# A graph network in one plan: setup reordered, later sign check, GpSimd booked longer, new priorities

## The chip, the cores and the metric

The kernel runs on one core of a Trainium2 chip. The metric is the device time of one execution in microseconds (us). The engines of the core are called PE (TensorE, matrix products), DVE (VectorE), ACT (ScalarE), POOL (GpSimd) and SP (SyncE, which here only issues transfers).

## The reference

Sixteen inputs of 1024 nodes with 256 features pass four layers over one 1024 x 1024 adjacency matrix of integers. Each layer adds its result to `x`, and each starts from `relu(layernorm(x))`. Layers 0 to 2 are graph attention, layer 3 is a transformer block:

```python
q = h @ W                                   # layer 0: 4 heads of 64; layers 1, 2: 1 head of 256
e = leaky(q @ a_src [i] + q @ a_dst [j])
x = x + act(softmax(where(adj > 0, e, -big)) @ q)     # elu, relu, elu
# layer 3: 8 heads of 32
t = softmax(where(adj > 0, q k^T / sqrt(32), -big)) @ v
y = layernorm(h + t);  y = layernorm(y + relu(y @ w1 + b1) @ w2 + b2);  x = x + y
```

## The kernel before

One core does all sixteen batches. `direct` does not emit instructions at once: it records pieces of work (`rec.add`) with an engine, an estimated duration and the buffers read and written. `Record.schedule` then plays a list schedule over the engines with these estimates and emits the pieces in the order that comes out. Each engine so has one fixed order, and semaphores on the buffers do the rest. Among the pieces ready on an engine the smallest key goes first. A key is the batch number plus a curve (`KNOTS`) over the position in its stream; `LEAD` shifts ACT's and DVE's keys, `BIAS` times `SWITCH` favours staying in PE's present packing, `PASS` is what passes until another engine sees a result, `SLACK` the same for transfers. A stream with a last argument of False has no lead.

The stages, by line of the kernel before:

- `setup` records `prepare(0)`, eight `neighbours`, `prepare(1)`, `prepare(2)` and the loads of the last layer's weights. `prepare` loads a layer's weights and multiplies them with the attention vector (DVE, L585 to L614). `neighbours` loads 128 rows of `adj` into a tile of `pa` (L623), makes flags of them in a second `pa` tile (DVE, L628), turns them on PE (L531) and copies them as bytes into `mask` (ACT, L646); DVE takes the least value of each row for a sign check (L655). The ring `r_pa` has six tiles.
- `begin` loads a batch (L1608) and takes sums and squares for its first layer norm on ACT (L1618, L448).
- `gat` is one graph layer. The inverse root is a power on POOL (L468 after squares, L483 after variances), DVE combines it with the mean (L475, L492), ACT writes the normalised rows `hn` (L502), PE turns them (L531) and multiplies with `w_aug` (L772). The exponentials `e` go through `rt` and `rd` and come back from memory spread over all partitions as `row` (L845, L854). DVE makes the weights `pt` (L870) from `row`, `e` and `mask`; PE multiplies them, in layer 0 by four column-packed matmuls at once (L984, L994), in layers 1 and 2 in 257 columns (L897, followed by DVE's reciprocal L917). POOL adds `e` to a running sum (L822).
- `attention` makes `qs` and `ks` (L1134 onwards), scores on PE (L1363) into four `sc` banks, exponentials on ACT (L1387), masks on DVE (L1396) and column-packed products with `va` (L1220). The tile `ks` is free until then.
- `feed` is the two-layer network of layer 3 (L1460) and the last layer norm.

The two first batches run layer 0 side by side; the second borrows tiles of the later layers for it (`lent`: `hTa`, `yT`, `xr`, `sums`, `pa`). After that every batch's graph layers are interleaved with the attention of an earlier one. All loads and stores but the running sums of `pa` (POOL, L1264) go through SP's queue, in the order of the plan.

Of the kernel before, what the change touches and what calls it, by code (L numbers as in the profile page):

```python
# [113 lines left out]


WEIGHT = {"pe": 1.0, "dve": 0.3}
PASS = {"pe": 0.146, "act": 0.223, "dve": 0.215, "pool": 0.13, "dma": 0.0}


class Work:  # L120
# [23 lines left out]
class Record:  # L144
# [135 lines left out]


BEHIND, HELD = 2.0, 1.35
SLACK = 0.871
KNOTS = {
    "gat0": (-9.618, -6.053, -5.32, -5.141, -2.375, -3.129, -0.814, -6.083, -6.096),
    "gat1": (-0.417, 0.283, 0.48, 0.671, 0.58, 0.798, 0.823, 0.86, 0.875),
    "gat2": (1.011, 0.044, -0.065, -1.338, 0.793, 0.704, 0.959, 1.386, 1.211),
    "beside": (-2.107, 2.085, 1.792, -1.66, 7.109),
    "values": (-0.174, -0.634, -1.621, -1.921, -0.925, 0.988, 7.017, 0.066, 0.002),
    "steps": (0.679, 1.306, 1.313, 1.627, 1.731, 1.892, 2.245, 2.072, 0.464),  # L290
    "feed": (2.531, 3.778, 2.14, 2.018, 2.622, 2.047, -0.257, 0.785, 3.186),
    "last": (1.057, 1.904, 1.664, 0.156, 2.035, 2.203, 2.695, 3.982, 5.043),
}
BIAS = 2.353
LEAD = {"act": 5.778, "dve": -2.572}

SWITCH = {
    ("full", "col4"): 0.137,
# [30 lines left out]
def direct(ctx, tc, flag, x, adj, gat_w, gat_a, w_qkv, ln1_g, ln1_b, ln2_g, ln2_b, w1, b1, w2, b2, out):  # L329
# [99 lines left out]
    def pool(us, emit, w, r):  # L429
        rec.add("pool", us, emit, w, r)  # L430

    def dma(moved, lands, emit, w, r, key=None, us=0.57, engine="dma"):
        rec.add(engine, us, emit, w, r, key=key, moved=moved, lands=lands)

    def stats(src, src_ref, dst, dst_ref, whose="g"):
# [19 lines left out]
    def inverse_of_squares(mean, squares, rstd, refs, rstd_ref, negate=True):  # L455

        n = squares.shape[-1]
        dve(
            ts_us(n),
            lambda: nc.vector.tensor_scalar(  # L460
                rstd, squares, 1.0 / C, EPS, op0=ALU.mult, op1=ALU.add
            ),
            [rstd_ref],
            refs,
        )
        pool(
            0.98,
            lambda: nc.gpsimd.tensor_tensor(  # L468
                out=rstd, in0=rstd, in1=neg_half[:, :n], op=ALU.pow
            ),  # L470
            [rstd_ref],
            [],
        )
        if negate:
            dve(tt_us(n), lambda: nc.vector.tensor_mul(mean, mean, rstd), refs, [rstd_ref])  # L475

    def inverse(mean, var, rstd, mv_refs, rstd_ref, negate=True):

        n = var.shape[-1]
        dve(ts_us(n), lambda: nc.vector.tensor_scalar_add(rstd, var, EPS), [rstd_ref], mv_refs)  # L480
        pool(
            0.98,
            lambda: nc.gpsimd.tensor_tensor(  # L483
                out=rstd, in0=rstd, in1=neg_half[:, :n], op=ALU.pow
            ),
            [rstd_ref],
            [],
        )
        if negate:
            dve(  # L490
                stt_us(n),
                lambda: nc.vector.scalar_tensor_tensor(  # L492
                    mean, mean, -1.0, rstd, op0=ALU.mult, op1=ALU.mult
                ),
                mv_refs,
                [rstd_ref],
            )
# [49 lines left out]


    b_aug = [Buf(t, []) for t in w_aug]
    b_mask, b_least, b_qkv, b_feed = (Buf(t, []) for t in (mask, least, wqkv_sb, w1_sb))  # L550

    def prepare(l):

        H = HEADS[l]
        D = C // H
        a_bc, aug = r_ota.new(), b_aug[l]
        dma(
            1.2,
            2.0,
            lambda: nc.sync.dma_start(  # L560
                w_aug[l][:, :, :C], gat_w[l].rearrange("(t p) d -> p t d", p=P)
            ),
            [aug],
            [],
        )
        dma(
            0.5,
            1.8,
            lambda: nc.sync.dma_start(
                a_bc.t.rearrange("p (s d) -> p s d", s=2)[:, :, :D],  # L570
                bass.AP(
                    tensor=gat_a[l].tensor, offset=gat_a[l].offset, ap=[[0, P], [D, 2], [1, D]]
                ),
            ),
            [a_bc],
            [],
        )
        for ct in range(CT):
            for s in range(2):
                tmp = r_ex.new()  # L580
                prod = tmp.t[:, :C].rearrange("p (h d) -> p h d", h=H)
                a_s = a_bc.t[:, s * C : s * C + D].rearrange("p (o d) -> p o d", o=1)
                dve(
                    tt_us(C),
                    lambda: nc.vector.tensor_mul(  # L585
                        prod,
                        w_aug[l][:, ct, :C].rearrange("p (h d) -> p h d", h=H),
                        a_s.to_broadcast([P, H, D]),
                    ),
                    [tmp],  # L590
                    [aug, a_bc],
                )
                to = C + (1 - s) * H
                dve(
                    tt_us(C),
                    lambda: nc.vector.tensor_reduce(
                        w_aug[l][:, ct, to : to + H], prod, AX.X, ALU.add
                    ),
                    [aug(("score", ct, s))],
                    [tmp],  # L600
                )
            wd = w_aug[l][:, ct, C : C + H]
            ws = w_aug[l][:, ct, C + H : C + 2 * H]
            dve(
                0.06,
                lambda: nc.vector.tensor_scalar_mul(
                    w_aug[l][:, ct, C + 2 * H : C + 3 * H], wd, ALPHA[l] - 1.0
                ),
                [aug(("low", ct))],
                [aug(("score", ct, 1))],  # L610
            )
            dve(
                0.06,
                lambda: nc.vector.tensor_scalar_mul(ws, ws, 1.0 - ALPHA[l]),  # L614
                [aug(("score", ct, 0))],
                [],
            )

    def neighbours(it):
        a32, nat = r_pa.new(), r_pa.new()  # L620
        a_i = a32.t.rearrange("p a n -> p (a n)").bitcast(I32)
        dma(
            1.8, 1.7, lambda: nc.sync.dma_start(a_i, adj[it * P : (it + 1) * P, :]), [a32], []  # L623
        )
        nat_f = nat.t.rearrange("p a n -> p (a n)")
        dve(
            ts_us(N),
            lambda: nc.vector.tensor_scalar(nat_f, a_i, 0.0, None, ALU.is_gt),  # L628
            [nat],
            [a32],  # L630
        )
        for j0 in range(0, NT, TH):
# [6 lines left out]
                    TH,  # L639
                ),  # L640
                [g],
                [nat],
            )
            act(
                act_us(HALF),
# [4 lines left out]
                [b_mask((it, j0))],  # L650
                [g],
            )
        dve(
            tt_us(N),
            lambda: nc.vector.tensor_reduce(least[:, it : it + 1], a_i, AX.X, ALU.min),  # L655
            [b_least(it)],
            [a32],
        )

    def mask_of(hf):  # L660
        return [b_mask((it, j0)) for it in range(hf * TH, (hf + 1) * TH) for j0 in (0, TH)]

    def setup():
        rec.stream(-3.0, (0.0, 1.0), False)
        prepare(0)
        rec.stream(-0.9, (0.0, 0.1), False)
        for it in range(NT):
            neighbours(it)
        rec.stream(-0.5, (0.0, 0.3), False)
        prepare(1)  # L670
        prepare(2)
# [2 lines left out]
            2.5,  # L674
            lambda: nc.sync.dma_start(wqkv_sb, w_qkv.rearrange("(t p) d -> p t d", p=P)),
            [b_qkv],
            [],
        )

        def load_feed():  # L680
# [4 lines left out]
            for n, ap in (("g2", ln2_g), ("c2", ln2_b)):  # L685
                nc.sync.dma_start(rows[n][:, 0, :], rows_on_all(ap, C))

        dma(5.0, 2.5, load_feed, [b_feed], [], us=5.7)

# [32 lines left out]
        )  # L724
        return rings

    def gat(xt, b_mv, b_rstd, l, my):
        H = HEADS[l]
        D = C // H
        mv, rstd = b_mv.t, b_rstd.t  # L730
# [5 lines left out]
        for hf in range(2):  # L736
            s = slice(hf * TH, (hf + 1) * TH)
            its = range(hf * TH, (hf + 1) * TH)
            mv_refs, rstd_ref = [b_mv((l, it)) for it in its], b_rstd((l, hf))
            inv = inverse_of_squares if l in SQUARED else inverse  # L740
            inv(mv[:, l, s, 0], mv[:, l, s, 1], rstd[:, l, s], mv_refs, rstd_ref)
            hn, hT = my.hn.new(), my.hT.new()
            for k, it in enumerate(its):
# [69 lines left out]
            if H == 1:  # L813
# [4 lines left out]
                    [b_e3(it) for it in its],  # L818
                )
            pool(  # L820
                0.686,
                lambda: nc.gpsimd.tensor_tensor(  # L822
                    out=sum_e[:, :, :H, s],
                    in0=sum_e[:, :, :H, s],
# [23 lines left out]
        def spread(hf, h, rd):  # L848
# [8 lines left out]
                    .rearrange("t n -> (t n)")  # L857
                    .partition_broadcast(P),
                ),
                [row],  # L860
                [rd],
            )
            return row

        def weights(hf, h, jt, row):
# [733 lines left out]
    def begin(b):  # L1599
        xt, b_mv, b_rstd = Halves(r_xh), r_mv.new(), r_rstd.new()  # L1600
        x_b = x[b].rearrange("(t p) c -> p t c", p=P)
        rec.stream(b, (0.0, 0.0), False)
        for hf in range(2):
            s = slice(hf * TH, (hf + 1) * TH)
            dma(
                1.8,
                3.0,
                lambda: nc.sync.dma_start(xt.half(hf), x_b[:, s, :]),  # L1608
                [xt(it) for it in range(hf * TH, (hf + 1) * TH)],
                [],  # L1610
                b - 1.0,
            )
        for hf in range(2):
            its = range(hf * TH, (hf + 1) * TH)
            for it in its:
                act(
                    act_us(C, 0, 1) + 95e-3,
# [13 lines left out]
            )  # L1631
        return xt, b_mv, b_rstd

    def graph(b, state, l, my=own, knots=None):
        rec.stream(b, knots or KNOTS[f"gat{l}"])
        gat(*state, l, my)

    def end(b, state):
        xt, x3 = state[0], r_x3.new()
# [11 lines left out]
        feed(b, x3, hn)  # L1651

    setup()
    states = [begin(0), begin(1)]
    graph(0, states[0], 0)
    borrowed = lent()
    graph(0, states[1], 0, borrowed, KNOTS["beside"])
    for r in vars(borrowed).values():
        if isinstance(r, Lent):
            r.give_back()  # L1660
    for b in range(NB):
        if b > 1:
            states.append(begin(b))
# [615 lines left out]
```

## Time and profile before

| | us |
|---|---|
| median of 3 runs | 4063.11 |
| lowest and highest | 4061.49, 4064.12 |
| the profiled execution | 4055.53 |
| its span | 4053.7 |
| PE busy in it | 3972.2 |
| DVE busy | 3624.3 |
| ACT busy | 2670.9 |
| POOL busy | 641.4 |

The span runs from the first to the last instruction of the core. The profile gives, for each engine, busy time, for each group of equal instructions its count, mean duration and the idle time just before it with the work that ended that idle time. The granted clock of PE was 0.997 of full speed over the span.

### The profile page before, as it was taken

The numbers are of one execution on the slowest core, as the hardware profiler recorded it, in microseconds if no ns is written. First come the engines' busy times: TensorE is split into PE (matmuls) and PEld (weight loads), VectorE is DVE, ScalarE is ACT, GpSimd is POOL, SyncE is SP. The second block draws the span as 40 slices with busy tenths as digits, with TensorE's granted clock in tenths as the row PEclk, the third lists the DMA queues.
The fourth block names the chain that finished last, engine by engine and source line by source line (L and its number), as shares of the span: only waits on it lengthen the run. The fifth ranks groups of instructions, "written<-read, shape, count | busy, mean of one in ns | idle before, by whom it ended". The sixth has DMA issues, their size and how long they took to land. (4 is left out here: it accounts for less than half of the span.)

```text
span 4053.7 us, 64966 instructions
## 1 busy us (share of the span) xinstructions
PE 3972.2 (98%) x23394; PEld 2337.5 (58%) x23394; DVE 3624.3 (89%) x6114; ACT 2670.9 (66%) x6673; POOL 641.4 (16%) x631
## 2 busy tenths in 40 slices
PE   7999999999999999999999999999999999999998
PEld 3566466564655646566565655646556465565653
DVE  7768998989989899999999989899898988989976
ACT  5467575675756766567675766757577665676675
POOL 1001121111112111111111211112021111211200
PEclk9999999999999999999999999999999999999999
DMA  4044453444544355453544535446444454535442
GB/s 129 24 118 110 119 137 98 120 104 117 138 106 117 92 128 123 111 135 80 136 111 120 136 90 129 99 117 141 103 115 99 122 129 107 134 82 124 117 127 57
DMA packets 227514, 456.46 MB, mean 113 GB/s; under 512 B 24688, under 2 KB 59760, under 8 KB 227184
## 3 DMA queue, kind: packets, MB, share of 16 engines
q1 hardware_dynamic: 192624, 326.39, 29.0%
q0 software_dynamic: 34560, 125.84, 16.2%
q8 instruction: 186, 3.05, 0.3%
q14 instruction: 144, 1.18, 0.1%
HBM read 225.25 MB, written 101.06 MB: 80 GB/s over the span
## 5 line engine op out<-in xcount | busy, mean ns | idle before, releaser
L1396 DVE TENSOR_TENSOR pa<-pa,mask 128x1024 f32<-128x1024 f32 x1024 | 1223.4, 1216 | 106.4 <-ACT pa L1387 106.3
L1387 ACT ACTIVATE pa<-sc 128x512 f32<-128x512 f32 x2048 | 1092.2, 600 | 229.2 <-PE sc L1363 146.0
L870 DVE SCALAR_TENSOR_TENSOR pt<-row,e,mask 128x512 f32<-128x512 f32 x1472 | 1006.4, 741 | 39.7 <-DMA row<-rd 22.7
L897 PE MATMUL bank<-qb,pt 128*128 128x257 f32 x4096 | 942.6, 381 | 3.5 <-DVE pt L870 3.3
L897 PEld LDWEIGHTS bank<-qb,pt 128*128 128x128 f32 x4096 | 769.3, 189 | 178.6 <-ACT ota L1303 12.6
L1363 PE MATMUL sc<-qs,ks 128*128 128x512 f32 x2048 | 739.3, 463 | 3.5 <-ACT pa L1387 3.4
L1220 PE MATMUL bank<-pa,va 128*32 128x512 f32 x4096 | 518.4, 598 | 0.2
L1363 PEld LDWEIGHTS sc<-qs,ks 128*128 128x128 f32 x2048 | 366.5, 189 | 220.9 <-issue 93.0
L984 PE MATMUL bank<-pt,qb 128*32 128x512 f32 x3840 | 459.8, 595 | 0.0
L1264 POOL DMA_DIRECT2D sums<-pa x240 | 213.9, 892 | 1464.5 <-DVE pa L1396 664.4
L925 ACT ACTIVATE ex<-bank,rec 128x256 f32<-128x256 f32 x256 | 121.3, 474 | 409.1 <-DVE rec L917 403.3
L772 PE MATMUL bank<-w_aug,hT 128*128 128x259 f32 (+1 forms) x1504 | 373.8, 390 | 0.7 <-ACT hT L766 0.7
L772 PEld LDWEIGHTS bank<-w_aug,hT 128*128 128x128 f32 x1504 | 276.7, 190 | 112.9 <-issue 33.6
L1247 DVE TENSOR_TENSOR sums<-pa,pa 128x1024 f32<-128x1024 f32 x240 | 289.1, 1217 | 9.9 <-PE bank L1220 9.9
L1255 DVE TENSOR_TENSOR sums<-sums,pa 128x1024 f32<-128x1024 f32 x240 | 290.9, 1213 | 1.6 <-DMA sums<-pa 1.6
L984 PEld LDWEIGHTS bank<-pt,qb 128*32 128x32 f32 x3840 | 120.3, 109 | 264.1 <-issue 218.5
L994 PE MATMUL bank<-pt,e 128*32 128x512 f32 x1920 | 251.2, 592 | 0.0
L1015 ACT COPY ot<-bank 128x512 f32<-128x512 f32 x120 | 68.5, 582 | 276.0 <-PE bank L984 262.9
L1134 PE MATMUL sc<-hTa,wqkv_sb 128*128 128x512 f32 x512 | 245.0, 601 | 3.0 <-ACT pa L1387 2.7
L1220 PEld LDWEIGHTS bank<-pa,va 128*32 128x32 f32 x4096 | 110.3, 109 | 237.1 <-issue 206.8
L502 ACT ACTIVATE hn<-xh,mv,rstd 128x256 f32<-128x256 f32 x376 | 199.1, 607 | 42.7 <-DVE mv L492 38.2
L448 ACT ACTIVATE waste<-xh,mv 128x256 f32<-128x256 f32 x384 | 196.1, 511 | 7.2
(153 smaller groups left out, 4608.6 us busy)
## 6 DMA issues: line engine op xcount, KB each, us to landing
sums<-pa POOLq DMA_DIRECT2D x240, 512.0 KB, 4.9
ks<-hl SPq DMA_DIRECT2D x256, 256.0 KB
qs<-hl SPq DMA_DIRECT2D x256, 256.0 KB
row<-rd SPq DMA_DIRECT2D x184, 256.0 KB
hl<-hi SPq DMA_DIRECT2D x128, 256.0 KB
hl<-lo SPq DMA_DIRECT2D x128, 256.0 KB
xh<-in_x_dram SPq DMA_DIRECT2D x32, 512.0 KB
x<-xh SPq DMA_DIRECT2D x32, 512.0 KB
```

The costliest lines, as they stand in the source:

```text
L772: nc.tensor.matmul(g.t[:, : C + 3 * H], hT.t[:, ct, k * P : (k + 1) * P], w_aug[l][:, ct, :], start=ct == 0, stop=ct == CT - 1,)
L870: lambda: nc.vector.scalar_tensor_tensor(pt.t, row.t, e3[:, 2, jt // TH, h, jt % TH : jt % TH + 1], mask[:, jt, hf * HALF : (hf + 1) * HAL ...
L897: nc.tensor.matmul(g.t[:, : D + 1], pts[jt].t[:, k * P : (k + 1) * P], qb[:, jt, 0, :], start=jt == 0, stop=jt == NT - 1,)
L984: nc.tensor.matmul(g.t[u * D + d : u * D + d + D3, :], qb[:, j, h + u, d : d + D3], pts[u][j - jt].t, start=j == 0, stop=j == NT - 1,)
L994: nc.tensor.matmul(gd.t[c : c + D3, :], one(jt + k, h + u).to_broadcast([P, D3]), pts[u][k].t, start=jt == 0, stop=jt == NT - 2,)
L1134: nc.tensor.matmul(sc.t, wqkv_sb[:, ct, c0 : c0 + P], hT.t[:, ct, hf * HALF : (hf + 1) * HALF], start=ct == 0, stop=ct == CT - 1,)
L1220: nc.tensor.matmul(ac.t[r * D3 : (r + 1) * D3, :], columns(r), of_head(r), start=first, stop=last,)
L1247: lambda: nc.vector.tensor_add(ss.t, p0.t, p1.t),
L1255: lambda: nc.vector.tensor_add(ss.t, ss.t, pt.t),
L1363: nc.tensor.matmul(scs[r - r0].t, ks.t[:, r, jt * P : (jt + 1) * P].bitcast(F32R), q.t[:, r, :].bitcast(F32R), start=True, stop=True,)
L1387: lambda: nc.scalar.activation(pt.t[:, v, :], sc.t, AF.Exp, scale=1.0 / math.sqrt(D3)),
L1396: lambda: nc.vector.tensor_mul(pt.t, pt.t, mask[:, jt : jt + 1, i0 : i0 + HALF].to_broadcast([P, 2, HALF]),),
```

## The change

Setup. The flags of `neighbours` go into the four parts of the tile `ks`, written as FP32R, and no longer into `pa`. The least values are taken later, in `signs`, from a second load of `adj` into `yT` tiles. `prepare(1)`, `prepare(2)` and the weight loads move to `setup_later`, recorded after batch 0's layer 0, and these loads and those of batches 1 and 2 are made to wait until the second, fourth or eighth `row` transfer has landed (`AFTER_ROWS`). Batch 0 takes its first statistics on DVE with `stats`, so its first inverse root goes the way of `inverse` (L480, L483, L492).

Plan. POOL's powers are booked with 1.6 in place of 0.98 us and its sums of `e` with 1.0 in place of 0.686, an SP issue with 0.42 in place of 0.57. `PASS`, `SLACK`, `KNOTS`, `BIAS` and `LEAD` have new values.

```diff
@@ -114,7 +114,7 @@
 WEIGHT = {"pe": 1.0, "dve": 0.3}
-PASS = {"pe": 0.146, "act": 0.223, "dve": 0.215, "pool": 0.13, "dma": 0.0}
+PASS = {"pe": 0.198, "act": 0.161, "dve": 0.218, "pool": 0.13, "dma": 0.0}
 
@@ -280,19 +280,19 @@
 BEHIND, HELD = 2.0, 1.35
-SLACK = 0.871
+SLACK = 0.944
 KNOTS = {
-    "gat0": (-9.618, -6.053, -5.32, -5.141, -2.375, -3.129, -0.814, -6.083, -6.096),
-    "gat1": (-0.417, 0.283, 0.48, 0.671, 0.58, 0.798, 0.823, 0.86, 0.875),
-    "gat2": (1.011, 0.044, -0.065, -1.338, 0.793, 0.704, 0.959, 1.386, 1.211),
-    "beside": (-2.107, 2.085, 1.792, -1.66, 7.109),
-    "values": (-0.174, -0.634, -1.621, -1.921, -0.925, 0.988, 7.017, 0.066, 0.002),
-    "steps": (0.679, 1.306, 1.313, 1.627, 1.731, 1.892, 2.245, 2.072, 0.464),
-    "feed": (2.531, 3.778, 2.14, 2.018, 2.622, 2.047, -0.257, 0.785, 3.186),
-    "last": (1.057, 1.904, 1.664, 0.156, 2.035, 2.203, 2.695, 3.982, 5.043),
+    "gat0": (-8.057, -7.567, -4.564, -6.528, -1.817, -1.899, -1.452, -3.246, -8.552),
+    "gat1": (-2.024, -0.004, 0.215, 0.731, 0.959, 0.704, 0.611, 0.917, 0.899),
+    "gat2": (1.118, -0.917, 0.633, 0.85, 0.97, 0.804, 1.307, 1.739, 1.201),
+    "beside": (-0.565, 3.144, 4.806, -3.201, 8.62),
+    "values": (-3.421, -4.341, -3.452, -4.286, -2.082, -2.123, 4.475, -0.299, 0.523),
+    "steps": (-0.249, 0.878, 1.095, 1.509, 1.61, 1.967, 1.973, 2.318, 0.345),
+    "feed": (4.232, 4.502, 1.869, 1.3, 2.54, 0.571, -2.425, 2.126, 2.697),
+    "last": (4.663, 0.548, 4.755, 0.436, 4.627, 5.109, 4.463, 6.627, 6.529),
 }
-BIAS = 2.353
-LEAD = {"act": 5.778, "dve": -2.572}
+BIAS = 4.008
+LEAD = {"act": 4.014, "dve": -5.116}
 
@@ -429,7 +429,7 @@
 
-    def dma(moved, lands, emit, w, r, key=None, us=0.57, engine="dma"):
+    def dma(moved, lands, emit, w, r, key=None, us=0.42, engine="dma"):
         rec.add(engine, us, emit, w, r, key=key, moved=moved, lands=lands)
@@ -464,7 +464,7 @@
         pool(
-            0.98,
+            1.6,
             lambda: nc.gpsimd.tensor_tensor(
@@ -479,7 +479,7 @@
         pool(
-            0.98,
+            1.6,
             lambda: nc.gpsimd.tensor_tensor(
@@ -547,7 +547,11 @@
     b_aug = [Buf(t, []) for t in w_aug]
+    rows_out = Buf(None, [])
+    n_rows = [0]
     b_mask, b_least, b_qkv, b_feed = (Buf(t, []) for t in (mask, least, wqkv_sb, w1_sb))
+
+    AFTER_ROWS = [[rows_out(n)] for n in range(8)]
 
@@ -561,7 +565,7 @@
             [aug],
-            [],
+            AFTER_ROWS[3] * (l > 0),
         )
@@ -573,7 +577,7 @@
             [a_bc],
-            [],
+            AFTER_ROWS[3] * (l > 0),
         )
@@ -616,17 +620,17 @@
 
-    def neighbours(it):
-        a32, nat = r_pa.new(), r_pa.new()
+    def neighbours(it, nat):
+        a32, part = r_pa.new(), nat(it % HG)
         a_i = a32.t.rearrange("p a n -> p (a n)").bitcast(I32)
...
         )
-        nat_f = nat.t.rearrange("p a n -> p (a n)")
+        nat_f = nat.t[:, it % HG, :]
         dve(
             ts_us(N),
-            lambda: nc.vector.tensor_scalar(nat_f, a_i, 0.0, None, ALU.is_gt),
-            [nat],
+            lambda: nc.vector.tensor_scalar(nat_f.bitcast(F32R), a_i, 0.0, None, ALU.is_gt),
+            [part],
             [a32],
@@ -639,7 +643,7 @@
                 [g],
-                [nat],
+                [part],
             )
@@ -650,22 +654,40 @@
             )
-        dve(
-            tt_us(N),
-            lambda: nc.vector.tensor_reduce(least[:, it : it + 1], a_i, AX.X, ALU.min),
-            [b_least(it)],
-            [a32],
-        )
+
+    def signs():
+
+        rec.stream(0, (0.9, 1.6), False)
+        for it in range(NT):
+            again = r_yT.new()
+            a_i = again.t.rearrange("p a n -> p (a n)").bitcast(I32)
+            dma(
+                1.8,
+                1.7,
+                lambda: nc.sync.dma_start(a_i, adj[it * P : (it + 1) * P, :]),
+                [again],
+                [],
+            )
+            dve(
+                tt_us(N),
+                lambda: nc.vector.tensor_reduce(least[:, it : it + 1], a_i, AX.X, ALU.min),
+                [b_least(it)],
+                [again],
+            )
 
...
         return [b_mask((it, j0)) for it in range(hf * TH, (hf + 1) * TH) for j0 in (0, TH)]
+
 
...
         rec.stream(-0.9, (0.0, 0.1), False)
+        nat = r_ks.new()
         for it in range(NT):
-            neighbours(it)
+            neighbours(it, nat)
+
+    def setup_later():
         rec.stream(-0.5, (0.0, 0.3), False)
@@ -674,7 +696,7 @@
             [b_qkv],
-            [],
+            AFTER_ROWS[7],
         )
@@ -685,7 +707,7 @@
 
-        dma(5.0, 2.5, load_feed, [b_feed], [], us=5.7)
+        dma(5.0, 2.5, load_feed, [b_feed], AFTER_ROWS[7], us=5.7)
 
@@ -724,7 +746,7 @@
 
-    def gat(xt, b_mv, b_rstd, l, my):
+    def gat(xt, b_mv, b_rstd, l, my, squared):
         H = HEADS[l]
@@ -737,7 +759,7 @@
             mv_refs, rstd_ref = [b_mv((l, it)) for it in its], b_rstd((l, hf))
-            inv = inverse_of_squares if l in SQUARED else inverse
+            inv = inverse_of_squares if squared else inverse
             inv(mv[:, l, s, 0], mv[:, l, s, 1], rstd[:, l, s], mv_refs, rstd_ref)
@@ -818,7 +840,7 @@
             pool(
-                0.686,
+                1.0,
                 lambda: nc.gpsimd.tensor_tensor(
@@ -857,9 +879,10 @@
                 ),
-                [row],
+                [row] + [rows_out(n_rows[0])] * (n_rows[0] < 8),
                 [rd],
             )
+            n_rows[0] += 1
             return row
@@ -1599,7 +1622,7 @@
         x_b = x[b].rearrange("(t p) c -> p t c", p=P)
-        rec.stream(b, (0.0, 0.0), False)
+        rec.stream(b, (0.0, 0.0) if b else (-5.0, -5.0), False)
         for hf in range(2):
@@ -1607,11 +1630,15 @@
                 [xt(it) for it in range(hf * TH, (hf + 1) * TH)],
-                [],
+                AFTER_ROWS[1 if b == 1 else 3] * (b in (1, 2)),
                 b - 1.0,
...
             its = range(hf * TH, (hf + 1) * TH)
+            if b == 0:
+                for it in its:
+                    stats(xt.at(it), xt(it), b_mv.t[:, 0, it, :], b_mv((0, it)))
+                continue
             for it in its:
@@ -1631,9 +1658,9 @@
 
-    def graph(b, state, l, my=own, knots=None):
+    def graph(b, state, l, my=own, knots=None, first=False):
         rec.stream(b, knots or KNOTS[f"gat{l}"])
-        gat(*state, l, my)
+        gat(*state, l, my, l in SQUARED and not first)
 
@@ -1651,13 +1678,16 @@
     setup()
-    states = [begin(0), begin(1)]
-    graph(0, states[0], 0)
+    states = [begin(0)]
+    graph(0, states[0], 0, first=True)
+    setup_later()
+    states.append(begin(1))
     borrowed = lent()
...
             r.give_back()
+    signs()
     for b in range(NB):
```

## Prediction

> **What bounds the kernel now.** I read the busy shares first, then the stretches of the setup, then who waited for whom in them, then the timeline, and last the steady part.
>
> ```profile
> PE 3972.2 (98%) x23394; PEld 2337.5 (58%) x23394; DVE 3624.3 (89%) x6114; ACT 2670.9 (66%) x6673; POOL 641.4 (16%) x631
> ```
>
> TensorE (PE) is the bound; only 81.5 us of the 4053.7 us span have no matmul at all. By stretch (columns: stretch, PE, weight loads, DVE, ACT, POOL, granted clock, DMA share, GB/s):
>
> ```profile
> 0.00:25.00 25.00, 11.30 (x41) 8.65 (x42) 14.95 (x46) 16.38 (x48) 2.44 (x9) 1.00 0.90 284
> 25.00:50.00 25.00, 16.46 (x86) 12.22 (x85) 18.78 (x36) 21.21 (x67) 2.52 (x4) 0.82 0.47 151
> 50.00:75.00 25.00, 23.59 (x179) 8.96 (x177) 17.76 (x36) 14.97 (x50) 3.74 (x4) 0.97 0.14 43
> 75.00:100.00 25.00, 22.26 (x193) 8.52 (x193) 25.00 (x49) 3.27 (x8) 4.61 (x2) 1.00 0.12 38
> ...
> 175.00:200.00 25.00, 25.00 (x193) 11.96 (x185) 19.52 (x33) 14.22 (x39) 1.93 (x3) 1.00 0.11 32
> ```
>
> The first 50 us lose 22.2 us of PE, more than a quarter of all its idle time; from 150 us on PE is full. The waits of PE in the first 60 us name the two that matter, and the timeline shows the second:
>
> ```profile
> PE bank L531 <- DVE pa L628: 12.5, 3, 11.5
> PE bank L531 <- ACT hTa L502: 6.1, 1, 6.1
> ```
>
> ```profile
> 39.02 20.68 SPq L854 DMA_DIRECT2D row<-rd  x3
> ...
> 43.80 0.16 DVE L475 TENSOR_TENSOR mv<-mv,rstd 128x4 f32<-128x4 f32 x1 [1.13 <-POOL rstd L468]
> 43.88 5.38 DVE L870 SCALAR_TENSOR_TENSOR pt<-row,e,mask 128x512 f32<-128x512 f32 x8
> ...
> 45.46 2.81 PE L531 MATMUL bank<-ident,hTa 128*128 128x128 f32 x8 [6.14 <-ACT hTa L502]
> ...
> 50.62 2.30 PE L984 MATMUL bank<-pt,qb 128*32 128x512 f32 x16
> ```
>
> The first weights `pt` are made at 43.88, behind batch 1's normalisation in DVE's queue; PE stands before batch 1's `hTa` transposes and starts the first graph product only at 50.62.
>
> For the steady part busy shares say little, so I took PE start to start from the timeline. A score matmul then steps by 0.231 us, a set of four column-packed ones by 0.429, one of the two passes of a 257-column product by 0.216, a transpose by 0.109. The span is then 11.5 (first matmul) + 3773 (work at these steps) + 103 (changes of packing) + 156 (stalls) + 10 (after the last matmul). Of the stalls 21 lie in 0 to 50 us, 8 in 50 to 150, 11 in the last 54, and the rest is some 7 us in each batch of about 247. Score visits hold 57 us of stalls in all: PE comes back for a `sc` bank before ACT has emptied it.
>
> **What the Trainium skill says.** "Perfetto Trace Analysis", Identifying the Most-Contended Engine, says that matmul busy share is no measure of headroom; the trace agrees: L1363 is busy 739.3 us for 2048 matmuls, 0.361 each against the step of 0.231. The same page, Tensor Engine Instruction, calls ACT, DVE and GpSimd strict FIFO; so L870 stood behind L475 above. "TensorE: Matmul & The Clock Gate", Part 1, puts the array at half clock after about 3.4 us of idleness; the trace agrees: 0.50 granted from 42 to 50 us, after 6.14 us of waiting. "DMA: Bandwidth & Descriptors", Bandwidth, gives 341 GB/s for 1 MB; here 284 to 418 GB/s over 4 to 18 us.
>
> **The change part by part.** From the built order of each engine; prices are rows of the profile.
>
> *Start of batch 0.* Its statistics leave ACT (8 x (0.432+0.206+0.511+0.192) + 2 x 0.222 = 11.2 us) for DVE (8 x (0.404+0.162) = 4.5 us). Eight sign reductions leave DVE's setup:
>
> ```profile
> L655 DVE TENSOR_REDUCE least<-pa 128x1 f32<-128x1024 int32 x8 | 9.7, 1211 | 0.0
> L870 DVE SCALAR_TENSOR_TENSOR pt<-row,e,mask 128x512 f32<-128x512 f32 x1472 | 1006.4, 741 | 39.7 <-DMA row<-rd 22.7 <-PE bank L994 10.8 <-PE bank L1220 2.8
> L468 POOL TENSOR_TENSOR rstd<-rstd,neg_half 128x4 f32<-128x4 f32 x96 | 155.5, 1620 | 221.3 <-DVE rstd L460 215.7 <-DVE rec L917 4.3
> ```
>
> and so do the products for layers 1 and 2 (8 x (0.419+0.413) + 8 x 0.148 = 7.8 us), which now come near the start of layer 1. Flags in `ks` leave all six `pa` tiles to the raw loads, so six of eight are issued before anything else, where three were. Walk: `x` lands at 7.9 as now; statistics 4.5 and three products 1.2 in between make 13.6; L480 0.15, POOL's power 1.73, L492 0.16: `hn` starts at about 15.6 instead of 18.6. From there to the issue of the first row the trace takes 32.03 - 18.58 = 13.5 us; a row issued at 57.97 was waited for until 61.68, 3.7 us. Now both first rows are issued together, ahead of the second half's `rd`. First `pt`: 15.6 + 13.5 + 3.7 = 32.8, 11 us earlier. Four `pt` (4 x 0.741) later PE starts products, about 36.2 instead of 50.6; batch 1's transposes, which it stood before, now come four groups later. It has done about 2 us less by then, so PE is 12 us ahead.
>
> Of that DVE, the pace of this stage (25.00 of 25 busy in 75 to 100), keeps what it can: its work from first `pt` to the first L917 reciprocal is 97.6 us by these rows before and 99.5 after (fewer `pt` of batch 1, but the 7.8 us of products). It took 43.9 to 148.0, so 148 - 11 + 2 = 139: 9 to 10 us earlier. I take **-10**; between -3 (DVE gains 11.4 and pays back the 7.8) and -14. Flags written as FP32R have no row: ACT's copy costs the same in that type (590 against 570 ns), so 0; at worst 1.2 us as a two-input pass of 1024 takes, 8 x 0.53 = +4.3.
>
> *Held loads.* `x` of batches 1 and 2 and the weights now wait on SP for a row to land. Behind them stand the next rows: eight issues of about 0.5 us for `load_feed` and batch 1's `rdl`. Cover: batch 0's layer 1 on PE. 0, at worst +3.
>
> *Late signs.* Eight loads of 512 KB and 9.7 us of DVE move to 170-260 us. Cover: DVE idles 5.5 us in 175 to 200 alone and 24.5 of 50 in 200 to 250, DMA share 0.11 to 0.27. DVE being FIFO, a late load would hold the work behind it: **+0.5**, 0 to +3.
>
> *Priorities, steady part.* The built order changes packing more often: full to column 192 to 180 (0.10 us each), column to full 284 to 299 (0.14), score to column 196 to 221 (0.095), column to score 104 to 102 (0.245): **+2.8**. Scores are more evenly spread: visits of four fell from 297 to 232, of two rose from 400 to 538. Between full-array work a visit of two stalled 0.014 us on the mean, one of four 0.124; before column work 0.02 and 0.18. With each class at its mean the 57 us become 48: **-9**, between -20 and +8, as the means hold only if neighbours keep their distance.
>
> *POOL booked at 1.6 instead of 0.98.* The rows say 1.62 and 1.73, so the plan errs less; DVE waits 33.7 + 17.0 us for these powers, off PE's path mostly: **-2**, 0 to -6. Sums at 1.0 likewise.
>
> *End.* One feed product of 1.98 us comes behind the last turn-back of `ota`, which heads the final 34 us: **-1.7**, -3 to +1.
>
> Sum: -10 + 0.5 + 2.8 - 9 - 2 - 1.7 = -19.4. The profiled execution took 4055.5 us (span 4053.7 and 1.8 around it), 7.6 below the median 4063.1; the sum gives 4036 for such a one and **4044** as a median.
>
> **Rivals.** *Slower, by a new wait in each batch.* Two stretches of a batch have DVE at 24.2 and 24.8 of 25 us already. If the new order puts `pt` and `pa` work into one stretch, PE waits for L870 or L1396 once per batch. It decides from 0.9 us in each of 14 batches, where it eats the 12 us of setup and end; at 2 us: -12 + 28, 4079. For it: all priorities changed at once; against it: the scores spread over 201 instead of 191 us of PE work in a batch.
> *No change.* DVE paces the setup, so an early PE start only moves its waits (-3), packing takes +2.8, and scores stall as before: 4063, with small parts 4056 to 4066. For it: 25.00 of 25 busy DVE; against it: DVE's own idle time ahead of 43.9.
> *More.* The stalls of 7 us in a batch shrink by 1.6 in each of 14: -22 beside setup and end, and with -2 for POOL 4027. For it: the plan's latencies and POOL times come nearer to the rows; against it: nothing shows which wait would go.
>
> **How the numbers follow.** 0.2% (8 us) is about what a measurement of this kernel can tell from no change. Forecast 0.56 (4032 to 4056), more 0.19 (4018 to 4032), no change 0.14, slower 0.11: faster 0.75, same 0.14, slower 0.11. The range 4020 to 4064 leaves out the slower case and the far end of the larger gain.
>
> **What would show it.** Right: first `pt` near 33 us and first graph product near 36; PE's idle time of the first 50 us down from 22 to about 15; first reciprocal of layer 1 (now L940) near 139; eight late reductions without a PE wait; fewer score stalls. Wrong: DVE busy before 33 us with flags near 1.2 us each; `pt` waiting for rows; a PE wait on `pt` or `pa` that returns every 240 us; batches longer than 247 us.

## Result and profile after

The changed kernel takes 4063.05 us (median of 14 runs, 4056.83 to 4067.75); the kernel before, beside it, 4061.71 us. The ratio is 1.0003, with a 95% interval of 0.9995 to 1.0012: no change where 19 us of gain were forecast. The profiled execution took 4064.2 us (span 4062.4), 1.2 above its median; the profiled one of before, 4055.5, was 6.2 below its own. So of the 8.7 us between the two spans some 7 are scatter of single executions, and the stage comparisons below, which rest on one execution each, must be read with that in mind.

The longest waits of PE in the first 60 us (us in total, times, longest), and the timeline of DVE and PE at the first weights (start, length, engine, line, operands, and in brackets the idle time before it):

```profile
PE bank L531 <- POOL rstd L483: 12.7, 1, 12.7
PE bank L794 <- ACT mask L650: 1.8, 1, 1.8
```

```profile
31.05 0.81 SPq L876 DMA_DIRECT2D row<-rd  x2
...
34.16 2.08 DVE L893 SCALAR_TENSOR_TENSOR pt<-row,e,mask 128x512 f32<-128x512 f32 x3 [1.62 <-DMA row<-rd]
...
35.06 1.05 PE L1007 MATMUL bank<-pt,qb 128*32 128x512 f32 x4 [0.91 <-ACT mask L650]
```

The 12.7 us are the wait for the first matmul of all, whose releaser is inferred. The early start works as forecast: the first `pt` comes at 34.16 us (43.88 before) and the first graph product at 35.06 (50.62), and PE no longer stands before batch 1's transposes (0.2 us in place of 6.1).

The groups of instructions that answer to those of before:

```profile
L673 DVE TENSOR_REDUCE least<-yT 128x1 f32<-128x1024 int32 x8 | 9.7, 1216 | 12.5 <-DMA yT<-in_adj_dram 12.5
L632 DVE TENSOR_SCALAR ks<-pa 128x1024 fp32r<-128x1024 int32 x8 | 5.5, 690 | 1.7 <-DMA pa<-in_adj_dram 1.7
L893 DVE SCALAR_TENSOR_TENSOR pt<-row,e,mask 128x512 f32<-128x512 f32 x1472 | 1008.0, 745 | 54.4 <-DMA row<-rd 38.9 <-PE bank L1017 13.4 <-PE bank L920 0.6
```

The flags cost the same in FP32R (690 ns on the mean; 684 before, as FP32). The sign reductions had no idle time before them; now DVE waits 12.5 us for their loads.

Where does the lead go? PE's waits from 60 to 150 us, and the timeline of the last two:

```profile
PE bank L794 <- DVE w_aug L618: 3.3, 1, 3.3
PE bank L860 <- DVE rec L1063: 3.2, 1, 3.2
PE bank L794 <- DVE w_aug L610: 2.8, 1, 2.8
PE bank L531 <- DVE rec L1063: 2.7, 1, 2.7
```

```profile
115.90 0.43 DVE L589 TENSOR_TENSOR ex<-w_aug,ota 128x256 f32<-128x256 f32 x1
...
120.34 0.15 DVE L610 TENSOR_SCALAR w_aug<-w_aug 128x1 f32<-128x1 f32 x1
...
120.55 0.70 PE L794 MATMUL bank<-w_aug,hT 128*128 128x259 f32 x2 [2.77 <-DVE w_aug L610]
...
124.36 0.15 DVE L618 TENSOR_SCALAR w_aug<-w_aug 128x1 f32<-128x1 f32 x1
...
124.50 5.04 PE L794 MATMUL bank<-w_aug,hT 128*128 128x259 f32 x14 [3.25 <-DVE w_aug L618]
```

The products for layer 1, whose loads were issued at 45.5 us, begin on DVE only at 115.90; PE comes for these very weights and waits twice. And windows of 25 us (PE, PEld, DVE, ACT, POOL busy, then the granted clock) show that PE is not at full clock in this stretch:

```profile
75.00:100.00 25.00, 21.84 (x157) 8.62 (x153) 22.39 (x46) 6.56 (x15) 2.12 (x2) 0.86 0.33 98
100.00:125.00 25.00, 18.85 (x163) 6.58 (x156) 19.95 (x53) 5.25 (x9) 2.21 (x2) 0.92 0.06 22
```

To compare stages I counted as in the prediction: PE's starts against its steps, packing changes apart; what is over is a stall, be it a wait or slower matmuls. Stages are cut by the matmul work done (of 3773 us), so that a row is the same amount of work in each kernel. The order of matmuls is that of the changed kernel in all but the first column, a few in the setup apart. Stalls in us, one profiled execution each (the last three are experiments, below):

| work done, us | before | changed | products early | signs left out | signs in gap |
|---|---|---|---|---|---|
| 0 to 40 | 24.1 | 9.7 | 9.8 | 9.3 | 11.7 |
| 40 to 80 | 4.9 | 11.1 | 11.5 | 6.3 | 13.0 |
| 80 to 90 | 0.1 | 8.8 | 0.1 | 9.9 | 0.1 |
| 90 to 200 | 2.7 | 3.9 | 4.2 | 3.4 | 3.8 |
| 200 to 300 | 12.4 | 19.2 | 17.8 | 12.3 | 12.3 |
| 300 to 3520 | 87.9 | 89.1 | 89.3 | 88.2 | 88.9 |
| 3520 to the end | 23.5 | 19.3 | 19.9 | 22.5 | 18.7 |
| changes of packing, whole span | 103.1 | 105.8 | 105.8 | 105.8 | 105.8 |

At 20 us of work the changed kernel is 13.0 us ahead (39.6 against 52.6), at 90 it is 1.8 behind, at 300 it is 9.6 behind.

From 300 to 3520 us of work the stalls hardly change, but they are not the same stalls. Some of PE's largest waits outside the setup (totals of the whole span), before and then in the changed kernel:

```profile
PE bank L1460 <- ACT ex L925: 13.5, 13, 1.0
PE bank L531 <- DVE rec L917: 9.8, 11, 1.2
```

```profile
PE bank L531 <- DVE yT L1521: 20.7, 16, 3.0
PE bank L794 <- ACT hT L788: 7.4, 16, 0.6
PE bank L1483 <- ACT ex L948: 4.7, 9, 1.5
```

The waits for `rec` and for `yT` stand before the same transposes, those of `yT` in `feed`: PE idles there for 20.8 us where it idled for 11.7, about once per batch, and up to 1.7 us at a time in the steady batches. The wait before the products of `feed` (L1460, now L1483) shrank by as much. The new order exchanged waits here and did not remove them.

### The profile page after: what moved, and what is told of

Same layout as the page of the kernel before. It is cut to its first block, busy times and chain, and to the rows that moved or that the text cites. A ratio compares the mean times of both kernels' runs of the same rounds, so it can differ in the third digit from the quotient of the medians.

```text
span 4062.4 us, 64901 instructions
## 1 busy us (share of the span) xinstructions
PE 3971.5 (98%) x23394; PEld 2330.7 (57%) x23394; DVE 3617.2 (89%) x6130; ACT 2666.1 (66%) x6639; POOL 718.9 (18%) x631
## 5 line engine op out<-in xcount | busy, mean ns | idle before, releaser
L1007 PE MATMUL bank<-pt,qb 128*32 128x512 f32 x3840 | 468.5, 598 | 2.7 <-DVE pt L893 1.5
L794 PE MATMUL bank<-w_aug,hT 128*128 128x259 f32 (+1 forms) x1504 | 388.6, 395 | 15.3 <-ACT hT L788 7.4
L468 POOL TENSOR_TENSOR rstd<-rstd,neg_half 128x4 f32<-128x4 f32 x94 | 159.2, 1694 | 747.6 <-DVE rstd L460 747.6
```

Of the source, the lines that this page charges most:

```text
L794: nc.tensor.matmul(g.t[:, : C + 3 * H], hT.t[:, ct, k * P : (k + 1) * P], w_aug[l][:, ct, :], start=ct == 0, stop=ct == CT - 1,)
L1007: nc.tensor.matmul(g.t[u * D + d : u * D + d + D3, :], qb[:, j, h + u, d : d + D3], pts[u][j - jt].t, start=j == 0, stop=j == NT - 1,)
```

## Experiments

My theory after the result: two separate losses eat the lead, the late products (work 80 to 90) and the late signs (200 to 300). The rivals were that DVE paces the setup wherever its work stands, that the stalls at the start of batch 0's attention belong to the new order, and that the new priorities eat a setup gain that passes through.

**products_early.** `prepare(1)`, `prepare(2)` move back:

```diff
     def setup():
         ...
             neighbours(it, nat)
+        rec.stream(-0.5, (0.0, 0.3), False)
+        prepare(1)
+        prepare(2)
     def setup_later():
         rec.stream(-0.5, (0.0, 0.3), False)
-        prepare(1)
-        prepare(2)
# in prepare, twice:
-            AFTER_ROWS[3] * (l > 0),
+            [],
```

> The changed kernel, but the weights of layers 1 and 2 are loaded, and their eight attention products made, in the setup again (ahead of the first pt, where DVE is idle for some 15 us) instead of at 115 us and later. TensorE's order is the same instruction for instruction. Theory A (the late products stand in DVE's fullest stretch and hold layer 1's first projections): the waits of PE on w_aug (2.8 + 3.3 us) and the 2.7 to 3.2 us of half clock around them go; about 8 us less, 4055 us. Rival B (DVE paces the setup wherever the 7.8 us of products stand): the first pt comes 6 to 8 us later than 34.2 and the time stays at 4063.

Measured: 4053.55 us, ratio to before 0.9979 (0.9973 to 0.9986). First `pt` at 34.08, not later. The first reciprocal of layer 1, changed kernel and experiment (line, count, least, median and longest ns, first and last start):

```profile
L940 DVE RECIPROCAL rec<-bank x256: 143/164/177, 146.4 to 3884.2; 128x1 f32<-128x1 f32 x128
```

```profile
L941 DVE RECIPROCAL rec<-bank x256: 135/159/169, 138.8 to 3876.0; 128x1 f32<-128x1 f32 x128
```

7.6 us earlier, with the same start; the trace shows no wait of PE from 110 to 140 us. The 7.8 us of products cost nothing ahead of the first `pt` because DVE waits for `e` there, 9.7 us in the changed kernel (L825). Theory A holds. Of the half clock only the part behind the two waits for `w_aug` went (the granted clock is 1.00 from 100 to 150 us); the part behind the two waits for L1063 stayed (0.88 and 0.91 in the two windows from 50 to 100 us).

**signs_emptied and early_signs_emptied.** The planned places stay, so the order does:

```diff
-                lambda: nc.sync.dma_start(a_i, adj[it * P : (it + 1) * P, :]),
+                lambda: None,
-                lambda: nc.vector.tensor_reduce(least[:, it : it + 1], a_i, AX.X, ALU.min),
+                lambda: nc.vector.memset(least[:, it : it + 1], 0.0),
```

> The changed kernel with its order kept, but the eight late sign loads (512 KB each) are left out and the eight reductions are replaced by tiny fills of the same 8 columns: the sign check is not computed. Theory A (the late signs hold DVE and crowd the DMA where batch 0's attention starts, 200 to 285 us): the 12.5 us of DVE waiting for these loads go, PE's stalls of 250 to 300 us fall from 16 to about 8, and the time falls by 6 to 8 us to about 4056. Rival B (these stalls belong to the start of batch 0's attention in the new order, signs or not): stalls of 250 to 300 us stay above 13, time 4061 to 4063.

> Both edits together: products of layers 1 and 2 early, and the sign check left out with the order kept. If the two losses are separate they add: 4063 - 8 - 7 = 4048. If the second stage only waits for what comes later anyway (the lead is given back at the start of batch 0's attention), the two together give no more than the better one, 4055.

Measured: 4056.22 us, 0.9993 (0.9985 to 1.0001), and 4046.89 us (6 runs), 0.9967 (0.9956 to 0.9979). The windows of 200 to 300 us, changed kernel and then without signs:

```profile
200.00:250.00 50.00, 47.98 (x250) 36.41 (x250) 34.53 (x84) 28.70 (x79) 4.42 (x8) 1.00 0.38 122
250.00:300.00 50.00, 43.26 (x175) 22.47 (x173) 33.00 (x35) 26.09 (x58) 3.87 (x5) 0.93 0.69 166
```

```profile
200.00:250.00 50.00, 48.41 (x250) 38.14 (x243) 24.65 (x79) 31.62 (x86) 3.90 (x7) 1.00 0.25 82
250.00:300.00 50.00, 46.23 (x202) 23.30 (x201) 41.68 (x45) 28.08 (x56) 3.87 (x5) 1.00 0.63 148
```

DVE's busy time looks better spread with the signs, and yet PE is busy for 3 us less in the second window, and runs at 0.93 of its clock there, which is another 3.5 us. Stalls of work 200 to 300 fall from 19.2 to 12.3 us, and beside products_early from 17.8 to 12.1; the kernel before has 12.4. In the changed kernel DVE stands 9.9 us before one sign's load:

```profile
258.47 1.22 DVE L673 TENSOR_REDUCE least<-yT 128x1 f32<-128x1024 int32 x1 [9.93 <-DMA yT<-in_adj_dram]
```

That load was issued at 249.68, between transfers to `ks` and `qs`, which fill this stretch in any case (the DMA share is 0.91 from 250 to 275 us, and 0.90 with the signs left out). The interval of signs_emptied overlaps that of the changed kernel, which was not in this set; what carries the price is early_signs_emptied beside products_early in one set, 6.7 us less between the medians (6.1 between means, give or take 1.8). The two losses add. No run separates what DVE's standing costs from what the second 4 MB of transfers cost.

**struct_only and plan_only.** The change in halves: the new setup with the old numbers, and the old setup with the new.

```diff
# struct_only: the changed kernel with
+BIAS = 2.353
+LEAD = {"act": 5.778, "dve": -2.572}
+SLACK = 0.871
# and KNOTS, PASS, the booked 0.98, 0.686 and dma us=0.57 of the kernel before
# plan_only: the kernel before with those of the changed one
```

> The changed setup (flags in ks, late signs, held loads, batch 0's statistics on DVE) with the priorities and booked times of the kernel before; from about 300 us on TensorE's order is that of the kernel before. Theory A (setup as a whole gains nothing, the new priorities cost 5 us in the steady batches and gain 8 at the end): 4063 + 8 - 5 = 4066. Rival B (the setup is worth its 10 us and the new priorities eat it): about 4052.

> The kernel before (its setup untouched) with the new priorities and booked times alone. Its built order changes packing far more often: 279, 350, 271 and 200 changes (full to column, column to full, score to column, column to score) where before has 192, 284, 196 and 104; at 0.10, 0.14, 0.095 and 0.245 us each that is 151.6 us against 103.1. Theory A (the priorities are fitted to one setup; off it they fall into an order of more changes, and each change is paid on TensorE): 4061 + 48 = 4109 us. Rival B (the changes are mostly hidden in waits, and the new priorities are better by themselves): below 4085.

Measured: 4086.98 us, 1.0066 (1.0053 to 1.0079), and 4217.38 us, 1.0389 (1.0373 to 1.0405). Both expectations missed in both. The packing changes of plan_only came as built (151.6 us), but its stalls rose by another 113 us, nearly all in the steady batches. struct_only loses 13 us in stalls between 340 and 400 us of work (48.0 to 60.7 in sum; 1 us in the changed kernel) and 5.3 us in one wait at the hand-over of the first batches:

```profile
PE sc L531 <- ACT pa L1410: 5.3, 1, 5.3
```

So the new numbers are no addition to the setup with a price of their own: on the new setup they are worth 24 us against the old ones, and with the old setup they cost 158 us.

**stats_act and flags_pa.** Single parts of the setup undone, the order kept:

```diff
# stats_act
-            if b == 0:
+            if False:
                 for it in its:
                     stats(...)
-        gat(*state, l, my, l in SQUARED and not first)
+        gat(*state, l, my, l in SQUARED)
# flags_pa
-        a32, part = r_pa.new(), nat(it % HG)
+        a32, part = r_pa.new(), r_pa.new()
```

> The changed kernel with one part undone: batch 0's first statistics on ACT again, not on DVE (TensorE's order is the same but for two places in the setup). Theory A (an early first pt is worth its time only as far as DVE, which paces the stage up to 130 us, can follow): first pt about 3 us later than 34.2, DVE has 4.5 us less to do before it, and of the 3 us at most 2 are left at 140 us: 4063 to 4065. Rival B (the start passes through in full): 4066 or more.

> The changed kernel with one part undone: the flags in pa tiles as FP32 again, so that three raw loads and not six are issued at once. Theory A as above: first pt 4 to 8 us later than 34.2, PE's idle time of the first 50 us up from 17 to about 22; half of it is still there at 140 us, 4066. Rival B (the late products hold layer 1 to 120 to 124 us whatever the start): the stalls there shrink by as much, 4063.

Measured: 4062.94 us, 1.0007 (1.0000 to 1.0013), and 4056.32 us, 0.9997 (0.9988 to 1.0005). With the statistics on ACT, the first `pt` comes at 38.3, 20 us of work are reached 4.1 us later, 90 us only 2.5 later, and the end is the same. With the flags in `pa` the first `pt` comes at 31.3, earlier than in either profiled execution of the changed kernel (34.2 and 32.8), and 20 us of work at 37.6 in place of 39.6: the expectation of a late first `pt` was wrong, and the time is no worse. So neither part shows a gain in the time. Of the early start the statistics earn about 4 us and the flags' new place nothing; which of the rest (sign reductions and products out of DVE's setup, rows issued together) earns what, no run shows.

**signs_in_gap** (three runs) and **products_early_2**, **after_2**. products_early with the sign check computed in full, at places where DVE waited for PE in the trace:

```diff
+        spare = [r_pa.tiles[k].rearrange("p a n -> p (a n)").bitcast(I32) for k in [0, 1, 4, 5]]
+        # look: the load of 128 rows into spare[it % 4]; judge: its least value
+        LOOK = {393: [0, 1, 2, 3], 545: [4], 574: [5], 588: [6], 597: [7]}
+        JUDGE = {545: [0], 574: [1], 588: [2], 597: [3], 611: [4], 672: [5], 734: [6, 7]}
+        for n, w in enumerate(rec.schedule()):
             w.emit()
+            # judge(it) for JUDGE[n], look(it) for LOOK[n]
```

> As products_early (products of layers 1 and 2 in the setup), and the sign check is computed again in full, but its eight loads go into four idle pa tiles from 95 us on, and its eight reductions stand at places of 143 to 205 us where DVE waited 1 to 3 us for TensorE; TensorE's order is that of the changed kernel. Theory A (the signs cost only by their place: DVE and DMA traffic at the start of batch 0's attention): all of what leaving them out gave comes back, 4047 us. Rival B (9.7 us of DVE and 4 MB of DMA cost the same wherever they stand): 4053 as products_early.

> The kernel of signs_in_gap once more, beside the two that follow: 4046 us, PE at half clock for 2 to 4 us after each of its two waits of 3.1 us near 70 and 92 us.

> The changed kernel once more, beside the next two: within 0.1% of the kernel before, as in its own runs.

> products_early beside the changed kernel on one chip. If the late products were held rightly for 9 to 10 us, 0.24% below after_2, and no layer-1 stall between 115 and 134 us.

> signs_in_gap beside products_early_2. Theory A (the place of the signs has a price, from DVE and DMA traffic where batch 0's attention starts): 5 to 7 us below products_early_2. Rival B (it has none; the first set of runs was lucky): within 2 us of products_early_2.

Measured: signs_in_gap 4046.29 us, 0.9968 (0.9956 to 0.9980), from 6 runs; again 4060.54 us, 0.9990 (0.9983 to 0.9997), from 21. These two intervals do not meet. The sets ran on different chips (11 and 0), but products_early and products_early_2 below ran on one chip, and their intervals do not meet either. So sets of runs differ by more than the intervals say. Hence the last set, all side by side on that chip: after_2 4071.85 us, 1.0017 (1.0009 to 1.0025); products_early_2 4063.71 us, 0.9998 (0.9990 to 1.0006); signs_in_gap_3 4060.95 us, 0.9987 (0.9980 to 0.9993). The early products are worth 8.1 us here (9.5 between the medians of the first sets). The first reciprocal came at 144.0 in after_2 and at 140.1 in products_early_2, a smaller step than the 7.6 us above, as stalls of work 40 to 80 vary by up to 5 us between executions of one order; those of work 80 to 90 are gone again. The place of the signs is worth 2.8 us by the medians (4.3 by the means, give or take 3.0): clear of nothing by the means, but not of the rival's 2 us, and short of theory A's 5 to 7 by the medians. Stalls of work 200 to 300 were 17.3 in products_early_2 and 13.6 in signs_in_gap_3; in the second run of signs_in_gap they were 15.8, with a granted clock of 0.93 from 250 to 300 us, where the first had 12.3 and 1.00. So part of the signs' stage is half clock that comes and goes. All three of the last set lost some 10 us more in the steady batches than in the earlier sets (98 to 100 us of stalls instead of 89), with the same order. About half of it lies before the transposes of `yT` (20.7 us of waits in the changed kernel, 25.4 in after_2); why is open.

**keep_warm and gap_flags_pa**, both from signs_in_gap:

```diff
             w.emit()
+            if n in (305, 384):
+                for _ in range(24):
+                    nc.tensor.transpose(r_sc.tiles[0][:, :P], ident, ident)
```

> signs_in_gap with 24 needless 128x128 transposes (0.109 us each, 2.6 us) ahead of each of TensorE's two waits for L1064 (3.11 us at 69 us and 3.24 us at 92 us); their results are not used. Theory A (the half clock after these waits costs 2.7 us each, 1.67 + 0.88 + 0.15 in the matmuls behind the first): granted clock 1.0 from 50 to 100 us, layer 1 up to 5 us earlier, 4042. Rival B (DVE paces this stage, so faster matmuls only wait longer for pt): 4046.

> signs_in_gap with the flags in pa tiles as FP32, as in the kernel before. flags_pa came out no slower than the changed kernel. Theory A (the early raw loads buy nothing once six of eight flags are in time): 4046 within 2. Rival B (the 2 us of the first product are worth their time): 4048 or more.

Measured beside signs_in_gap_2 (4060.54): keep_warm 4054.04 us, 6.5 less (6.4 between means, give or take 2.8), ratio to before 0.9977 (0.9969 to 0.9984); gap_flags_pa 4059.46 us, the same (0.2 less, give or take 3.4). The timelines of PE in signs_in_gap, in its second run, and in keep_warm:

```profile
71.88 1.97 PE L531 MATMUL bank<-ident,hTa 128*128 128x128 f32 x8 [3.11 <-DVE rec L1064]
73.64 0.42 PE L861 MATMUL bank<-ident,xr 128*16 128x128 f32 x1
73.99 3.57 PE L1008 MATMUL bank<-pt,qb 128*32 128x512 f32 x16
```

```profile
68.86 1.09 PE L531 MATMUL bank<-ident,hTa 128*128 128x128 f32 x8 [3.11 <-DVE rec L1064]
69.78 0.27 PE L861 MATMUL bank<-ident,xr 128*16 128x128 f32 x1
70.19 1.93 PE L1008 MATMUL bank<-pt,qb 128*32 128x512 f32 x16
```

```profile
67.68 2.78 PE L1713 MATMUL sc<-ident 128*128 128x128 f32 x24
70.96 1.09 PE L531 MATMUL bank<-ident,hTa 128*128 128x128 f32 x8 [0.50 <-DVE rec L1064]
71.89 0.27 PE L861 MATMUL bank<-ident,xr 128*16 128x128 f32 x1
72.30 1.92 PE L1008 MATMUL bank<-pt,qb 128*32 128x512 f32 x16
```

The same wait of 3.11 us is followed by half clock in one execution (16 products in 3.57 us) and not in the other (1.93). With the filler the wait shrinks to 0.50 and the products run at full clock.

That the 6.5 us come from there is not shown. The profiled execution of signs_in_gap_2, which is 8.3 us longer than that of keep_warm, had full clock behind both waits too:

```profile
50.00:75.00 25.00, 21.76 (x177) 9.34 (x169) 20.16 (x45) 16.40 (x53) 4.73 (x4) 1.00 0.09 34
75.00:100.00 25.00, 22.00 (x185) 9.27 (x181) 24.70 (x47) 6.55 (x15) 1.98 (x2) 1.00 0.56 182
```

The two executions are level at 300 us of work (357.5 us, and 358.0 in keep_warm), and part only in the steady batches, where no filler stands (about 100 us of stalls, and 91). The granted clocks of all executions allow an estimate of the clock's part: on the mean 0.9961 in 21 executions of signs_in_gap_2 and 0.9968 in 16 of keep_warm, which is 2.5 us of 4060; each is on record to 0.001 only. Among the executions at 0.997 or more (10 and 12) keep_warm is still faster, 4053.0 us against 4056.5. keep_warm computes everything and is the fastest of its set, 0.23% below the kernel before beside it; the changed kernel was not in this set.

## Why the prediction was wrong

Step by step, by the profiled executions:

| step | forecast, us | measured, us |
|---|---|---|
| start: 20 us of work done | -12 | -13.0 |
| from there to layer 1 (90 us of work) | +2 | +14.8 |
| signs and start of attention (to 300) | +0.5 | +7.8 |
| steady batches (to 3520): packing, scores, POOL | +2.8 -9 -2 | +4.3 |
| end | -1.7 | -4.5 |

- **Right: the start.** First `pt` 34.16 for 32.8, first product 35.06 for 36.2, PE idle in the first 50 us 16.8 for 15; flags in FP32R free. One part was credited wrongly: six raw loads issued at once were to help, and with the flags back in `pa` the start was no later (flags_pa).
- **Wrong: "148 - 11 + 2 = 139".** The first reciprocal came at 146.4. I treated DVE's stage as a sum of work and put the 7.8 us of products anywhere in it. But taking them from ahead of the first `pt` relieved nothing, as DVE waits there for `e`; and where they went, PE waits for exactly their result. products_early gives 138.8 by undoing this one move. That this is the forecast number is luck, as executions of that order of PE came at 133.4 to 142.0. I had bounded the step at -3 with the 7.8 paid back, and missed the dependency and the clock behind it. The remaining 6 us (work 40 to 80) are waits for L1063, which stands behind `pt` in DVE's queue (5.9 us; 3.7 for the same line before), and half clock after them, which came in some executions of this order and not in others.
- **Wrong: late signs "+0.5".** The cover was read off the windows of before. In the changed kernel the loads fall where `ks` and `qs` are moved, and a late load holds all of DVE's work behind it. Leaving the signs out takes 5.7 to 6.9 us off the stage's stalls; moving them is worth 2.8 us of the time by the medians.
- **Wrong: scores "-9".** The visits were counted rightly, but the mean of a class did not keep: visits of two between full-array work went from 0.014 to 0.093 us (354 of them), visits of four from 0.124 to 0.026. In sum score visits took 102.4 us with their packing changes where they took 101.0. And a term was missing: of PE's waits in a batch I priced the score visits alone and put the others at nothing. The one at the transposes of `yT` grew by 9 us, while the one before the products of `feed` shrank by 9.
- **Right: packing.** +2.7 for +2.8; the built changes are paid at the steps read from before, whose medians are the same in the changed kernel to 1 ns.
- **POOL "-2": no gain seen.** DVE's waits for L468 fell from 33.7 to 3.2 us and those for L483 from 17.0 to 12.6, but DVE's waits for ACT's squares (L460) rose from 10.9 to 29.8, and PE's steady stalls did not fall. No run isolates it.
- **The rival "no change" came out**, partly for its reason: packing and scores as it said, and the lead lost in DVE's stage; the price of the signs was in neither. The rival "slower" has its wait that returns in each batch, at `yT` and not at `pt` or `pa`, and paid for by another that shrank.

The Trainium skill's page "TensorE: Matmul & The Clock Gate", Part 1, says that the window of the clock gate runs freely, so that the cold part differs between runs. These traces agree (3.57 against 1.93 us above). They also show the drop after waits of 2.74 to 3.25 us, so the 3.4 us of the prediction is no limit below which PE is safe.

## What to carry to other kernels

Price moved work by who waits for its result at the new place and who waited for the engine at the old one; a sum of busy time hides both. Priorities fitted to a plan belong to that plan: change the work and its numbers together, and price them together. Stalls per class of visit are a property of the order they were measured in. When an edit gains time, look in which stage the time was gained before naming its cause.

## What the runs showed of the hardware

A wait of about 3 us on PE can cost 2.7 us more in the matmuls after it (0.88, 0.15 and 1.64 us in the three lines shown for signs_in_gap and its second run), by chance from execution to execution. With a filler of 2.78 us ahead of each of two such waits, they shrank to 0.50 and 0.61 us and the clock stayed at 1.00; how much of the 6.5 us between the medians this gave is open. Sets of runs of one kernel differed by up to 14 us in the median (signs_in_gap, 4046.29 and 4060.54, on two chips) and by 10 on one chip (products_early, 4053.55 and 4063.71), while the kernel before, measured in the same sets, moved by 6 and by 4. So only kernels beside each other can be compared at this size.
